# Layer 0 of a four-layer net: three PSUM bank pairs in a ring, both score halves in a row, head mixing behind the product with v

## The chip, the cores and the metric

The kernel runs on one core of a Trainium2 chip. A core has five engines that work beside each other, each through its own instructions in order: TensorE (matmuls; the profile calls it PE and its weight loads PEld), VectorE (DVE), ScalarE (ACT), GpSimd (POOL) and SyncE (SP, which here only issues transfers). Sixteen DMA engines move data. TensorE writes to PSUM, a memory of eight banks of 512 fp32 per partition; ScalarE and VectorE read it. The metric is the time of one execution on the device in microseconds, lower is better. A difference of about 0.2% is what a measurement of this kernel can tell from none.

## The reference

A batch of four images with 512 channels and 32 x 32 positions goes through four residual layers, each on a group-normalized input. The change concerns layer 0, an attention with talking heads:

```python
xf = x.reshape(b, c, t)                         # t = 1024
q, k, v = (einsum('oc,bct->bot', w, xf) ... )   # 8 heads of 64
attn = einsum('bhdq,bhdT->bhqT', q, k) * scale
attn = einsum('gh,bhqT->bgqT', w_head, attn)    # heads mixed before the softmax
attn = softmax(attn, axis=-1)
attn = (attn - mean) / sqrt(var + EPS)          # one mean and var per image and head
attn = attn * in_gamma + in_beta
out = einsum('bhqT,bhdT->bhqd', attn, v)
out = out.reshape(b, t, c) @ w_proj.T + b_proj
```

The layers after it (a small quantum-circuit gate, a second attention, a memory with the best 8 of 2048 items) follow in the same kernel and are not touched. All arithmetic is in fp32.

## The kernel before, in words

Layer 0 works image by image, and an image in 32 steps (`STEPS`) of 32 queries each. `step` (L1164) writes out the order of a step by hand: nearly every instruction goes through `pin` (L55), which keeps the written order on its engine. So what stands first in `step` runs first on its engine, and a waiting instruction holds back everything behind it on that engine.

For one step s the data goes this way:

- `scores(b, s, n)` (L436), for each half n of the keys: eight matmuls of q with k fill a pair of PSUM banks, and ScalarE copies the pair into the SBUF tile `ss`. After the second half the scores are relayed into the tile `s2` (the profile says `s`) by eight DMAs, four issued by SP and four by GpSimd (L462). They turn partitions around so that heads lie beside each other. `s2` has two buffers, so the relay of step s writes where the mixing of step s-2 has read.
- `mix` (L465), two steps later: 16 matmuls with the small matrix `wmix` mix the heads, into two pairs of banks (`mx0`, `mx1`).
- `exps` (L475): ScalarE takes the exponential of each pair into one half of the tile `e`, which has one buffer.
- `turn_keys` (L479): VectorE transposes a half of `e` into `eT`, which has two buffers of four steps each (a tile of 128 queries).
- `reduce` (L488): VectorE takes statistics of `e` (eight `bn_stats`), for the softmax's sums and the variance.
- `apply` (L500): TensorE multiplies `eT` with v into the bank `pv`, in four parts per tile, `LAG` = 6 steps behind the scores. `take_out` (L570) copies the finished bank.
- `sums` (L517): a generator that goes on by a piece at each `next`. GpSimd adds the statistics, TensorE sums them over partitions into the small bank `pt`, VectorE takes the reciprocal, GpSimd sends it through DRAM to spread it (`rb`), and `scale` (L574) multiplies with it on GpSimd.

Eight banks hold all this: the pairs `sc`, `mx0`, `mx1`, and the single banks `pv` and `pt`. Both score halves of a step use the one pair `sc`; the order on TensorE is first scores, mixing of step s-2, second scores, small-bank work, product with v, and then a `piece`.

What fills a `piece` (L1244) depends on the step. In steps 0 to 6 it is `take_v`, the projection of a further tile of v. From step 12 to 27 of images 1 to 3 it is `put_quarter` (L673), a quarter of the output projection of the image before, into the bank `pt`, added to the image by VectorE. In the other steps there is nothing, or small work for the next image's norm. `mid` (L1223) and `early` (L1214) carry further small work: sums of v at steps 7 and 8, the loads of the image pieces `xr` and their stores, the instance norm of the image before, group-norm coefficients, and the loads for the next image, which ScalarE issues in steps 28 to 31. After step 31 come `LAG` steps without scores, four of which hold a q projection of the next image, then its k projections.

Of the kernel before, what the change touches and what calls it, by code (L numbers as in the profile page):

```python
# [10 lines left out]
F32 = mybir.dt.float32  # L11
# [30 lines left out]
def fast_net(ctx: ExitStack, tc: tile.TileContext, a: dict, out: bass.AP, flag: bass.AP):  # L42
# [9 lines left out]
    pairs = {at: ps_a.tile([P, 2, NB], F32, tag=at, name=at) for at in ("sc", "mx0", "mx1")}  # L52
# [124 lines left out]
    def place(at, name):  # L177

        return pairs[at] if at else ps_s.tile([P, 2, NB], F32, tag="sc", name=name)
# [46 lines left out]
    LAG = 6  # L226
# [57 lines left out]
    def first():  # L284
# [35 lines left out]
        def multiply(k, m):  # L320
            for n in range(T // NB):
                pin(nc.tensor.matmul(
                    pairs[f"mx{m}"][:, n, :],
                    w[:, k, m * P:(m + 1) * P], xn[:, k, n * NB:(n + 1) * NB],
                    start=(k == 0), stop=(k == KC - 1),
                ))
# [18 lines left out]
        for m in range(2):  # L345
            put_q(q, m)(flat2(pairs[f"mx{m}"]))
        for m, at in ((2, "sc"), (3, "mx0")):
            project(w, tokens(xn), m, at, put_q(q, m))
# [24 lines left out]
    def normalized(b, scale, bias):  # L373

        xn = img[b]["xn"]
        for ks in ((), (), (0,), (1, 2), (3,)):
            for k in ks:
                pin(nc.scalar.activation(
                    xn[:, k, :], xn[:, k, :], AF.Identity,
                    bias=bias[:, k:k + 1], scale=scale[:, k:k + 1],  # L380
                ))
            yield
# [53 lines left out]
    def scores(b, s, n):  # L436
# [7 lines left out]
        sc = pairs["sc"]  # L444
# [19 lines left out]

    def mix(b, s):  # L465
        s2 = img[b].pop(("s2", s))
        for t in range(4):
            for r in range(4):
                pin(nc.tensor.matmul(  # L469
                    pairs[f"mx{r // 2}"][t * NS:(t + 1) * NS, r % 2, :].rearrange("p (qq k) -> p qq k", qq=2),  # L470
                    wmix[r * NS:(r + 1) * NS], s2[r * NS:(r + 1) * NS, :, t * NK:(t + 1) * NK],
                    start=True, stop=True,
                ))

    def exps(s, half):  # L475
        pin(nc.scalar.activation(  # L476
            e[:, half].rearrange("p r qq k -> p (r qq k)"), flat2(pairs[f"mx{half}"]), AF.Exp))
# [10 lines left out]
    def reduce(b, s):  # L488

        I = img[b]  # L490
        j, i = divmod(s, 4)
        if i == 0:
            I["st", j] = apool.tile([P, 4, 4, 2, 6], F32, tag="st", bufs=2, name=f"st_{b}_{j}")
        st = I["st", j]
        for half in range(2):
            for r in range(2):
                for qq in range(2):
                    pin(nc.vector.bn_stats(st[:, i, 2 * half + r, qq, :], e[:, half, r, qq, :]))  # L498
# [662 lines left out]
    for m, at in enumerate(("mx1", "sc", "mx0", "mx1")):  # L1161
        take_k(0, m, at)

    def step(b, s, mid, piece):  # L1164
# [3 lines left out]
        old = s - 2  # L1168
        j, part = divmod(s - LAG, 4)
        tiled = 0 <= j < TC  # L1170
        if tiled and part == 0:
            I["tail"] = sums(b, j)
            next(I["tail"])
# [5 lines left out]
        if 0 <= old < STEPS:  # L1179
            mix(b, old)  # L1180
            exps(old, 0)
            turn_keys(old, 0)
        elif s < STEPS:
            piece(b, s)
        if s < STEPS:
            scores(b, s, 1)
        if 0 <= old < STEPS:
            exps(old, 1)
        if tiled and part == 0:
            next(I["tail"])  # L1190
        mid(b, s)
        if tiled:
            apply(b, s - LAG)
            if part == 3:
                take_out(b, j)
        if 0 <= old < STEPS:
            turn_keys(old, 1)
            reduce(b, old)
        if old >= 0:
            piece(b, s)  # L1200
        if tiled and part < 3:
            next(I["tail"], None)
# [20 lines left out]
    def mid(b, s):  # L1223
# [5 lines left out]
        if b > 0:  # L1229
            if s == 3:  # L1230
                state["norm"] = instance_norm(before)
            if 3 <= s < 7 or OUT - 2 <= s <= OUT:
                next(state["norm"], None)
            if OUT <= s + 1 < OUT + 16 and s % 2:
                image_piece(before, (s + 1 - OUT) // 4, (s + 1 - OUT) // 2 % 2)
            if OUT < s <= OUT + 16 and s % 2 == 0:
                piece_out(before, (s - 2 - OUT) // 4, (s - 2 - OUT) // 2 % 2)
            if s == NEXT:
                state["behind"] = chain(state["behind"], gating(before))
        if NEXT - 3 <= s:  # L1240
            next(state["ahead"])
        next(state["behind"], None)

    def piece(b, s):  # L1244
# [4 lines left out]
        if TC < s < NEXT - 3 and not state["held"]:  # L1249
            state["held"] = next(state["ahead"]) is True  # L1250

    for b in range(B):
# [12 lines left out]
        places = dict(zip(range(STEPS, STEPS + KC), ("sc", "sc", "mx0", "mx1")))  # L1265
        for s in range(STEPS, STEPS + LAG):
            step(b, s, lambda b, s: next(state["behind"], None),
                 lambda b, s: qs[s - STEPS](places[s]) if s in places else None)
# [5 lines left out]
        for m, at in enumerate(("sc", "mx0", "mx1", "mx0")):  # L1274
            ks[m](at)
        if last:
# [3 lines left out]
            for i, at in enumerate(("mx0", "mx1", "sc", "mx0")):  # L1280
                take_v2(0, i, at)
            for m, at in enumerate(("mx1", "sc", "mx0", "mx1")):
                put_out(b, m, at)
# [799 lines left out]
```

## Time and profile before

| what | value |
|---|---|
| median of 3 runs | 2703.63 us (2702.09 to 2707.51) |
| the profiled execution | 2704.59 us, its span 2702.8 us |
| granted TensorE clock, mean | 0.987 |
| busy: PE, PEld | 2574.9 us (95%), 1143.7 us (42%) |
| busy: DVE, ACT, POOL | 1496.9 (55%), 1007.4 (37%), 1234.5 us (46%) |
| steps of image 0, first scores to last scores' start | 74.12 to 278.19 us |
| the same for images 1, 2, 3 | 358.55 to 589.47, 671.02 to 901.41, 987.08 to 1218.42 us |

Busy time is what the profile shows between an instruction's start and its modelled end; matmuls overlap, so a busy TensorE need not be at its peak. A group of instructions is named by its line, engine, operation and tiles, output before input: `sc<-k,q` are the scores, `mx<-s,wmix` the mixing, `pv<-eT,v` the product with v, `pt<-of,w_p` a projection quarter, `ss<-sc` the copy of scores, `e<-mx` the exponential. Square brackets in a timeline hold the engine's idle time before a row and what ended it. The mean over the span hides that the steps differ; so stretches of it are asked for by themselves.

### The profile page before, as it was taken

The page shows a single profiled execution, that of the slowest core. Times are in us where ns is not written, and L with a number is a line of the kernel's source. Part 1 is how long each engine was busy: PE and PEld are TensorE (multiplying, and loading weights), DVE is VectorE, ACT ScalarE, POOL GpSimd, SP SyncE. Part 2 cuts the span into 40 slices and gives each one's busy share as a digit, 9 for nine tenths or more (in the row PEclk, how much of TensorE's full clock was granted, in tenths as well). Part 3 has the DMA queues.
Part 4 walks back from the last instruction along what each step waited for, and adds up shares of the span by engine and source line. Part 5 has one row for each costly group of instructions (what it writes and reads, how often), then busy time and mean ns, then how long its engine had stood idle before and what let it go on. Part 6 is the DMA issues. An engine that isn't in the chain of part 4 may idle for free.

```text
span 2702.8 us, 47004 instructions
## 1 busy us (share of the span) xinstructions
PE 2574.9 (95%) x18286; PEld 1143.7 (42%) x18286; DVE 1496.9 (55%) x2386; ACT 1007.4 (37%) x1149; POOL 1234.5 (46%) x1891
## 2 busy tenths in 40 slices
PE   8998999989999898989999999999999999999995
PEld 3343434544345443545433443343344344444442
DVE  4497337871588416873246225424513437878886
ACT  1565336551565325652145035214403622121211
POOL 2266425552466415554067027205602626666664
PEclk9999999999999999999999999999999999999997
DMA  2477437770587527675310030021002016766665
GB/s 79 126 212 211 126 94 224 222 217 28 170 234 208 154 67 197 200 209 197 121 44 1 31 125 1 16 81 60 1 32 93 1 56 190 217 190 215 183 183 161
DMA packets 159320, 349.81 MB, mean 129 GB/s; under 512 B 32361, under 2 KB 65129, under 8 KB 155378
## 3 DMA queue, kind: packets, MB, share of 16 engines
q1 hardware_dynamic: 88608, 167.17, 20.1%
q0 software_dynamic: 49152, 142.79, 18.5%
q10 hardware_dynamic: 21330, 36.76, 4.6%
q8 instruction: 147, 2.41, 0.4%
q14 instruction: 83, 0.68, 0.1%
HBM read 178.57 MB, written 33.69 MB: 79 GB/s over the span
## 4 chain that ended last, share of the span: by engine, by line
PE 81%; DMA 6%; ACT 5%; DVE 3%; POOL 2%; issue 2%; SPq 1%; ACTq 0%; POOLq 0%; DVEq 0%
PE at L1096 16%; PE sc_c L975 8%; PE pv_c L1008 8%; PE mx L193 7%; PE sc L447 7%; PE pv L509 6%; DMA s<-ss 4%; PE p L193 4%; ACT ss L453 4%; PE sc L193 4%; PE pt L406 4%; PE q L193 3%; PE k L193 3%; PE v L205 3%; PE pt L682 3%
## 5 line engine op out<-in xcount | busy, mean ns | idle before, releaser
L482 DVE STREAM_TRANSPOSE eT<-e 128x1024 f32<-128x1024 f32 x256 | 316.9, 1241 | 261.5 <-ACT e L476 259.5
L462 POOL DMA_DIRECT2D s<-ss x512 | 259.4, 515 | 364.9 <-ACT ss L453 283.7
L1113 POOL DMA_INDIRECT got<-in_mem,ix x256 | 278.4, 1087 | 217.2 <-DVE tmx L1119 94.1
L453 ACT COPY ss<-sc 128x1024 f32<-128x1024 f32 x256 | 259.0, 1012 | 254.8 <-PE sc L447 205.7
L969 ACT ACTIVATE eT<-sc_c 128x1024 f32<-128x1024 f32 x256 | 247.8, 1022 | 278.8 <-PE sc_c L975 216.9
L498 DVE BATCH_NORM_STATS2 st<-e 128x6 f32<-128x256 f32 x1024 | 341.6, 405 | 0.0
L993 POOL TENSOR_TENSOR e<-eT 128x1024 f32<-128x1024 f32 x96 | 230.1, 2398 | 177.7 <-ACT eT L969 147.0
L447 PE MATMUL sc<-k,q 64*32 64x512 f32 x4096 | 284.0, 610 | 19.8 <-ACT ss L453 14.6
L476 ACT ACTIVATE e<-mx 128x1024 f32<-128x1024 f32 x256 | 262.4, 1028 | 65.2 <-PE mx L469 28.0
L994 DVE TENSOR_TENSOR eT<-eT,e 128x1024 f32<-128x1024 f32 x96 | 131.5, 1370 | 249.5 <-POOL e L993 249.3
L509 PE MATMUL pv<-eT,v 128*64 128x128 f32 x4096 | 254.2, 278 | 0.0
L509 PEld LDWEIGHTS pv<-eT,v 128*64 128x64 f32 x4096 | 223.8, 138 | 61.5 <-issue 59.9
L975 PE MATMUL sc_c<-q,k 64*128 64x512 f32 x1024 | 238.8, 606 | 2.5 <-DVE xr L648 2.3
L989 POOL TENSOR_TENSOR eT<-eT 128x1024 f32<-128x1024 f32 x32 | 80.6, 2520 | 348.6 <-ACT eT L969 335.8
L1008 PE MATMUL pv_c<-eT,v 128*64 128x512 f32 x1024 | 232.2, 596 | 0.0
L469 PE MATMUL mx<-s,wmix 32*32 32x512 f32 x4096 | 157.3, 620 | 39.8 <-DMA s<-ss 39.8
L1137 DVE SCALAR_TENSOR_TENSOR acc<-got,et,acc 128x512 f32<-128x512 f32 x224 | 168.5, 752 | 8.0
L1035 DVE RECIPROCAL ri_c<-ri_c 128x512 f32<-128x512 f32 x32 | 107.1, 3345 | 96.1 <-ACT ri_c L1034 96.1
L975 PEld LDWEIGHTS sc_c<-q,k 64*128 64x128 f32 x1024 | 94.4, 187 | 132.1 <-issue 73.5
L1101 ACT COPY att<-at 128x1024 f32<-128x1024 f32 x64 | 64.8, 1012 | 217.6 <-PE at L1096 217.5
L585 POOL TENSOR_TENSOR o<-pv,rb 64x256 f32<-64x256 f32 x128 | 111.2, 869 | 66.2 <-ACT pv L572 59.2
L1008 PEld LDWEIGHTS pv_c<-eT,v 128*64 128x64 f32 x1024 | 70.5, 137 | 152.6 <-issue 151.4
(316 smaller groups left out, 3231.5 us busy)
## 6 DMA issues: line engine op xcount, KB each, us to landing
s<-ss SPq DMA_DIRECT2D x512, 128.0 KB
s<-ss POOLq DMA_DIRECT2D x512, 128.0 KB, 4.0
rb<-r POOLq DMA_DIRECT2D x64, 128.0 KB, 5.4
o<-o SPq DMA_DIRECT2D x32, 256.0 KB
xr<-in_x ACTq DMA_DIRECT2D x32, 256.0 KB
x<-xr SPq DMA_DIRECT2D x32, 256.0 KB
xr_c<-x SPq DMA_DIRECT2D x32, 256.0 KB
x<-xr_c SPq DMA_DIRECT2D x32, 256.0 KB
```

The lines of the kernel that those rows point to most:

```text
L193: pin(nc.tensor.matmul(ps[:, n, :], w[:, k, m * P:(m + 1) * P], rhs(k, n), start=(k == 0), stop=(k == KC - 1),))
L447: pin(nc.tensor.matmul(sc[m * NS:(m + 1) * NS, r, :], q[r * HD:(r + 1) * HD, m, s * NS:(s + 1) * NS], k_[r * HD:(r + 1) * HD, m, n * NB:(n ...
L453: pin(nc.scalar.copy(ss[:, :, n * NB:(n + 1) * NB], sc))
L462: pin(relays[side].dma_start(out=s2[2 * m + r::NH], in_=ss[m * NS:(m + 1) * NS, r, :]))
L476: pin(nc.scalar.activation(e[:, half].rearrange("p r qq k -> p (r qq k)"), flat2(pairs[f"mx{half}"]), AF.Exp))
L482: pin(nc.vector.transpose(eT[:, j % 2].rearrange("p b (qq i r) x -> p i r qq b x", qq=2, i=4)[:, i, 2 * half:2 * half + 2], e[:, half].rea ...
L498: pin(nc.vector.bn_stats(st[:, i, 2 * half + r, qq, :], e[:, half, r, qq, :]))
L509: pin(nc.tensor.matmul(pv[r * HD:(r + 1) * HD, gp, :], I["v"][:, t, g * HD:(g + 1) * HD], eT[:, j % 2, t, :, 4 * g:4 * g + 4], start=(t == ...
L975: pin(nc.tensor.matmul(sc[:, r, :], I["k"][r * HD:(r + 1) * HD, m, t * P:(t + 1) * P], I["q"][r * HD:(r + 1) * HD, m, n * NB:(n + 1) * NB] ...
L1008: pin(nc.tensor.matmul(pv[r * HD:(r + 1) * HD, :], I["v"][:, t, h * HD:(h + 1) * HD], e[:, r, :], start=(t == 0), stop=(t == TC - 1),))
L1096: pin(nc.tensor.matmul(sc[:, n * NB:(n + 1) * NB], xn3[b][:, k, tt * P:(tt + 1) * P], memT[k][:, i0:i0 + NB], start=(k == 0), stop=(k == K ...
L1113: pin(nc.gpsimd.indirect_dma_start(out=got[:, i, :], out_offset=None, in_=a["mem"], in_offset=bass.IndirectOffsetOnAxis(ap=ix[:, i:i + 1], ...
```

## The change

Three things are reordered, with no matmul added or left out.

The three pairs of banks become a ring without fixed roles. Score half n of step s takes pair (s+n) mod 3; the mixed half h in step s takes pair (s+2+h) mod 3. So within a step the second mixed half reuses the pair of the first scores, and the next step's second scores reuse the pair of the first mixed half.

The order in a step is now: both score halves; the sums matmul; in steps with a projection quarter, `mid`; the product with v; the mixing; both exponentials; in other steps `mid`; the `piece`.

VectorE's work for the second half of `e` (transpose and four statistics) is put off to the next step, behind that step's small-bank work. Because of that, the sums of a tile begin at step 4j+6 and their matmul stands in step 4j+7, and the product lags by 7 steps instead of 6. The copy of `pv` stands behind both exponentials. The store of an image piece (`piece_out`) moves to the start of a step, its load (`image_piece`) behind the copy of `pv`, and the small norm work for the next image starts one step earlier.

```diff
-    pairs = {at: ps_a.tile([P, 2, NB], F32, tag=at, name=at) for at in ("sc", "mx0", "mx1")}
+    pairs = [ps_a.tile([P, 2, NB], F32, tag=f"pair{i}", name=f"pair{i}") for i in range(3)]
...
-    LAG = 6
+    MIX = 2
+    SUM = 6
+    LAG = 7
...
-        sc = pairs["sc"]
+        sc = pairs[(s + n) % 3]
...
+    def mixed(s, half):
+        return pairs[(s + MIX + 2 + half) % 3]
...
     def step(b, s, mid, piece):
         I = img[b]
-        old = s - 2
+        old = s - MIX
+        mixing = 0 <= old < STEPS
+        js, at = divmod(s - SUM, 4)
+        summing = 0 <= js < TC
         j, part = divmod(s - LAG, 4)
         tiled = 0 <= j < TC
-        if tiled and part == 0:
-            I["tail"] = sums(b, j)
-            next(I["tail"])
+        putting = b > 0 and OUT <= s < OUT + 16
+        if b > 0 and OUT < s <= OUT + 16 and s % 2 == 0:
+            piece_out(b - 1, (s - 2 - OUT) // 4, (s - 2 - OUT) // 2 % 2)
         if s == 0:
             take_v(b, 0)
         if s < STEPS:
             scores(b, s, 0)
             early(b, s)
-        if 0 <= old < STEPS:
+            scores(b, s, 1)
+        if summing and at == 1:
+            next(I["tail"])
+        if putting:
+            mid(b, s)
+        if s >= MIX and "late" in I:
+            turn_keys(I["late"], 1)
+            reduce(b, I.pop("late"), 1)
+        if summing and at == 0:
+            I["tail"] = sums(b, js)
+            next(I["tail"])
+        if tiled:
+            apply(b, s - LAG)
+        else:
+            piece(b, s)
+        if mixing:
             mix(b, old)
             exps(old, 0)
+            exps(old, 1)
             turn_keys(old, 0)
-        elif s < STEPS:
-            piece(b, s)
-        if s < STEPS:
-            scores(b, s, 1)
-        if 0 <= old < STEPS:
-            exps(old, 1)
-        if tiled and part == 0:
-            next(I["tail"])
-        mid(b, s)
-        if tiled:
-            apply(b, s - LAG)
-            if part == 3:
-                take_out(b, j)
-        if 0 <= old < STEPS:
-            turn_keys(old, 1)
-            reduce(b, old)
-        if old >= 0:
-            piece(b, s)
-        if tiled and part < 3:
+        if tiled and part == 3:
+            take_out(b, j)
+        if b > 0 and OUT <= s + 1 < OUT + 16 and s % 2:
+            image_piece(b - 1, (s + 1 - OUT) // 4, (s + 1 - OUT) // 2 % 2)
+        if not putting:
+            mid(b, s)
+        if tiled:
+            piece(b, s)
+        if mixing:
+            reduce(b, old, 0)
+            I["late"] = old
+        if summing and at > 0:
             next(I["tail"], None)
```

The rest of the diff gives the projections of q, k and v and the first image's start their places in the ring by number, gives `reduce` the half as an argument, and moves the two image-piece calls out of `mid`.

## The prediction, made before the changed kernel ran

> **What bounds the kernel now.** I read the page first: TensorE is busy 95% of the span, so a change must either take TensorE's waits away or shorten its sequence. The change touches layer 0 alone, which the timeline puts between 74 and about 1290 us. So I asked next for TensorE's waits in that stretch:
>
> ```profile
> PE mx L469 <- DMA s<-ss: 39.8, 18, 6.5
> PE pt L533 <- POOL sums L530: 14.8, 12, 2.2
> PE sc L447 <- ACT ss L453: 14.6, 19, 1.5
> ```
>
> The columns are total us, times, longest. The mixing waits for its relayed scores, the small sums matmul for GpSimd, the scores for ScalarE's copy of the half before. All rows together give about 78 us: what waiting alone could return. Then the timeline of one step of image 1 with a projection quarter, TensorE's rows and the copy:
>
> ```profile
> 460.54 1.09 PE L447 MATMUL sc<-k,q 64*32 64x512 f32 x16
> ...
> 461.55 1.20 PE L469 MATMUL mx<-s,wmix 32*32 32x512 f32 x32
> 461.73 1.01 ACT L453 COPY ss<-sc 128x1024 f32<-128x1024 f32 x1 [2.36 <-PE sc L447]
> ...
> 462.80 1.09 PE L447 MATMUL sc<-k,q 64*32 64x512 f32 x16
> 462.90 1.02 ACT L476 ACTIVATE e<-mx 128x1024 f32<-128x1024 f32 x1 [0.15 <-PE mx L469]
> ```
>
> Start to start: first scores 1.02, mixing 1.24, second scores 1.02, product with v 1.90, quarter 1.93: 7.11 us, and most of steps 13 to 24 of images 1 to 3 take exactly that. Such steps are TensorE's own length, hardly any waiting. "Bare" steps, with neither a projection nor a quarter (image 0 from step 9; steps 9 to 11 and 28 to 31 elsewhere), are 5.18 at best. In image 0 they are far from it, and one call with stretches shows why; columns are length, busy PE, PEld, DVE, ACT, POOL, then clock, DMA share, GB/s:
>
> ```profile
> 149.75:248.50 98.75, 87.73 (x1580) 42.74 (x1579) 89.93 (x186) 65.42 (x70) 71.65 (x158) 0.98 0.76 222
> 570.00:575.00 5.00, 4.96 (x96) 2.32 (x96) 4.46 (x12) 3.33 (x4) 3.33 (x10) 1.00 1.06 256
> 575.00:580.00 5.00, 1.29 (x20) 0.19 (x16) 4.45 (x10) 1.83 (x3) 2.18 (x4) 0.99 1.05 262
> 580.00:585.00 5.00, 2.70 (x40) 0.57 (x48) 0.22 (x1) 1.51 (x2) 2.81 (x7) 0.50 0.75 221
> ```
>
> VectorE is 91% busy in image 0; and where the next image's loads run (570 to 580) the DMA engines are full, TensorE stands still, and its clock is 0.50 after that. One more row, from image 0, for the sums:
>
> ```profile
> 172.71 0.41 PE L533 MATMUL pt<-sums,same 128*128 128x32 f32 x2 [1.59 <-POOL sums L530]
> ```
>
> The second scores began at 170.00, so this matmul comes 2.71 after them instead of 1.02.
>
> **What the skill says.** TensorEngine Tiling (Array Packing), Key Properties: a change of tiling mode drains TensorE. The trace agrees: the scores' second pass starts 0.453 after the first and would leave the array free 0.91 after the block's start, yet the mixing (other tile shape) comes at 1.02. TensorE: Matmul & The Clock Gate, Part 1: after an idle window of about 3.4 us the clock is halved. It agrees: after 5.73 us of waiting the mixing at 582.30 took 2.02 instead of 1.20. DMA: Bandwidth & Descriptors, Anatomy of one DMA: a semaphore wait for a DMA is done on the issuing sequencer. So GpSimd's queue stands still while a relay waits; GpSimd's 283.7 us of waits for the copy, on the page, fit.
>
> **The change, part by part**, summed against the profiled run (2704.6 us, span 2702.8; median of the runs 2703.6, so the same within 0.04%).
>
> (a) *Scores side by side.* One mode change of five goes (1.02 to 0.91: 0.11), and the wait of second scores for the first copy goes. The mixing's second pass would free the array at about 1.04, with a drain of 0.11 at 1.15; it now takes 1.24: 0.09. Step with a quarter: 0.91+1.02+1.90+1.15+1.93 = 6.91, so 0.20 less. 48 such steps (12 to 27 of three images): -9.6.
>
> (b) *Steps 0 and 1* have no mixing to lie between the score halves. TensorE waits 1.17 us for the copy at each step's end, from 78.77 to 81.03. With the ring: 0.91+1.02+3.63 (v) = 5.56 for 6.91: -1.35 x 8 = -10.8.
>
> (c) *A new wait.* The second scores take the pair that the previous step's first mixed half leaves, so they wait for its exponential. That begins 1.35 after the mixing's start (461.55 to 462.90), takes 1.02, and 0.06 later scores may start: 2.43 after the mixing. With the quarter between they come only at 1.15+1.93+0.91 = 3.99: hidden. In a bare step they would come at 2.06: 0.37 of stall, and the loop is 2.43+1.02+1.90 = 5.35, over 5.18. In steps 2 to 6 (v instead of the product) 2.43+1.02+3.63 = 7.08 for 6.95: +0.13 x 20 = +2.6. Steps 7 and 8 have the sums of v behind the mixing, which hides it: -0.15 x 8 = -1.2.
>
> (d) *Sums a step later.* GpSimd adds in step 4j+6, the matmul stands behind the next step's scores, VectorE's second half and its statistics are done early. The 14.8 us should nearly go. In bare steps 0.3 stays: GpSimd issues four relays (2.0) before the add (0.29), done about 2.4 after the mixing's end, where the matmul would come at 2.25.
>
> (e) *Bare steps of image 0.* Steps 9 to 28 took 120.25 us, 6.01 each. VectorE needs 89.93 in the 16 steps of the stretch shown with a small edge, near 5.5 each; the loop of (c) 5.35 plus a quarter of sums (0.33+0.3) and of the pv copy (0.59), which now stands behind both exponentials: 5.65. I take 5.70: -0.31 x 20 = -6.2. Bounds: 5.5 (-10) and no gain.
>
> (f) *Relays.* Their issue now waits for the mixing of two steps before, later in the same step; in return the mixing is late too. Issue on GpSimd 2.05, landing median 4.0, longest 9.5 (page and tile view). Time from the end of one mixing to the next use of its buffer: 2 x 6.91 - 1.2 = 12.6, less 2.3 of issue and signals leaves 10.3 for landing. Before, copy end (4.45 into the step) to mixing two steps on (1.02): 8.4. In bare steps: 2 x 5.5 - 3.6 = 7.4 against about 5. So about 2 us more room. Queued behind the waiting relay are, on GpSimd, the sums and the scaling (some 2.3 us a step, waited for by TensorE in (d) only), on SP the stores of o and x, which none waits for soon. Steps 9 to 11 of images 1 to 3 took 61.9 us, 7.9 of it DMA waits in TensorE's list; at 5.7 and half the waits 55.3: -6.6. Steps 28 to 31: the mixing of step 30 waits 4.7 to 6.6 us, and stands 2.8 later in its step, which would take 2.8 and some of the slow clock; but the engines are full there, so half of 14 comes back in the next step: -7. Bounds 0 and -20.
>
> (g) *Small-bank work and sums in the quarter steps.* Those 48 steps take 353.7; at 7.11 they are 341.3, plus 4 of sums matmuls: 8.4 is waits and small matmuls around steps 12, 22 and 25 to 28. I let 40% go: -3.4. VectorE needs 88.67 us of 103.34 there, 6.1 of 7.1 a step, so 6.9 is still open to it. The image piece is now loaded behind the exponentials: 7 us before its add instead of 12, which the landing times cover.
>
> (h) One step more of lag adds no instructions to TensorE's tail, where projections fill it: 0. If the product had to wait for VectorE at steps 35 to 38 it would cost some 1 us per image. The bank names in the first and last projections: 0, the copies there have 7 us projections as cover.
>
> Sum: -9.6-10.8+2.6-1.2-6.2-6.6-7.0-3.4 = -42.2, so 2661.4 of the median; I say 2662.
>
> **Rivals.** *The freed time is taken back*: VectorE at 91% and full DMA engines set the pace, so (e), (f) give nothing and (a), (g) half: -10.8+1.4-6.5 = -16, 2688. For it: the stretches shown. Against it: VectorE's 5.5 is under 6.01, and its second half is now ready work for idle moments.
>
> *The DMA waits go*: 2.8 us more room ends the half clock too; (f) gives 20 and 10, (e) 10: -62, 2642. For it: each wait is a single event per image. Against: the engines are already full at 262 GB/s there.
>
> *Slower*: the ring ties TensorE to VectorE. Its place is the first exponential, which waits for `e` to be read (25.6 us of such waits before), and the second scores now wait for that exponential without the whole step that lay between. If VectorE's delays add to the 5.35 loop, the 44 bare steps grow. Gains (a) and (b), less the rest of (c), are 19, and (g)'s 3.4: 22.4 in all, so it decides from 0.5 us per bare step over before, at about 6.5 in image 0; at 7.0 it is +22, 2726. For it: image 0 runs at 6.01 with a floor of 5.18, so adding happens already. Against: the second half no longer stands between two first halves.
>
> That the change does not do what it says is excluded: in the built order TensorE has both score halves, product, mixing, quarter.
>
> **How the numbers follow.** Forecast 0.58 (2645 to 2680), taken back 0.18 (2680 to 2698), waits gone 0.09 (2638 to 2645), no change 0.05, slower 0.10. About 0.2%, 5 us, is what a measurement can tell from no change. Range 2640 to 2697: it leaves out most of the slower case and some of no change. Faster 0.85, same 0.05, slower 0.10.
>
> **What would show it.** Step starts 6.9 apart with quarters, 5.6 in steps 0 and 1, near 5.7 in bare steps of image 0; no scores row waiting for the copy, a new one waiting for the exponential, some 0.3 each in bare and v steps; sums under 4 us; DMA waits of the mixing near 25 instead of 39.8. I am wrong if the exponential's row passes 30 us, if VectorE is idle while bare steps stay at 6.0, or if the relays land later and the DMA row grows.

## The result, and the profile after

The changed kernel takes 2700.89 us, median of 20 runs (2690.16 to 2705.93), where the kernel before took 2704.90, median of 20 runs beside them (2699.03 to 2713.91). The ratio is 0.9978, 95% interval 0.9968 to 0.9989: some 6 us faster, just about what can be measured. The forecast was 2662, with a range of 2640 to 2697: the kernel gave back nearly all of what it should have gained.

First the page of the changed kernel, busy time, share of the span and instructions of each engine:

```profile
PE 2581.5 (96%) x18286; PEld 1156.0 (43%) x18286; DVE 1483.1 (55%) x2387; ACT 996.4 (37%) x1148; POOL 1236.2 (46%) x1891
```

TensorE has the same 18286 matmuls and is busy 6.6 us *longer* than before. The mean clock of this profiled execution is 0.979, that of the one before 0.987, but the two lie at the edges of what the kernels show. Over its 20 runs the changed kernel has 0.979 to 0.983, median 0.9815. The kernel before has 0.982 to 0.987, median 0.984, in the 15 runs made beside the first experiments. By the medians the loss of clock is 0.0025 of 2702 us, some 7 us of work (an estimate); the two profiles alone would make it 22.

The list of TensorE's waits in layer 0 (74 to 1300 us) has the same columns as before, total us, times, longest:

```profile
PE pair L475 <- DMA s<-ss: 29.7, 11, 4.8
PE pt L538 <- POOL sums L535: 20.3, 10, 5.1
PE pair L449 <- ACT e L482: 9.5, 38, 1.5
```

The mixing's waits for relayed scores fell, from 39.8 to 29.7. The scores' wait for the exponential is the new one of step (c), at 0.25 each time. But the row of the sums, which was to go nearly to nothing, grew from 14.8 to 20.3, and its longest wait from 2.2 to 5.1. The sum of all rows is 78.3 us, as before. The list does not hold every stop, though: it has those between TensorE's matmuls, and a matmul's modelled end can hide a stop inside a block.

Such a stop came with the ring. The mixing's second half now writes the pair that the first scores of the same step used, so it waits for ScalarE's copy of them. It is seen in the list of TensorE's weight loads, before and then after:

```profile
PEld mx L469 <- ACT ss L453: 1.7, 1, 1.7
```

```profile
PEld pair L475 <- ACT ss L455: 14.5, 26, 0.9
```

One step of image 1 with a projection quarter, in the timeline:

```profile
519.59 1.95 PE L449 MATMUL pair<-k,q 64*32 64x512 f32 x32
521.47 1.97 PE L514 MATMUL pv<-eT,v 128*64 128x128 f32 x32
523.36 1.14 PE L475 MATMUL pair<-s,wmix 32*32 32x512 f32 x32
524.43 1.99 PE L687 MATMUL pt<-of,w_p 128*128 128x256 f32 x8
...
526.36 1.09 PE L449 MATMUL pair<-k,q 64*32 64x512 f32 x16
```

From start to start: both score halves 1.88, product 1.89, mixing 1.07, quarter 1.93: 6.77 us where it was 7.11. That is 0.34 less a step, where (a) had forecast 0.20.

So I cut the span at the starts of scores and put stretch beside stretch. All numbers are us, each from one profiled execution, sums over the images named:

| stretch | before | after | forecast | measured |
|---|---|---|---|---|
| up to the first scores | 74.1 | 74.1 | 0 | 0.0 |
| steps 0 and 1, all images | 55.3 | 44.1 | -10.8 | -11.2 |
| steps 2 to 8, all images | 211.7 | 203.8 | +1.4 | -7.9, less 7.6 moved: -0.3 |
| steps 9 to 28, image 0 | 120.2 | 125.2 | -6.2 | +5.0 |
| steps 9 to 11, images 1 to 3 | 61.9 | 73.7 | -6.6 | +11.8 |
| steps 12 to 27, images 1 to 3 | 353.7 | 337.6 | -13.0 | -16.1 |
| from there to the next image or the end | 1825.9 | 1843.6 | -7.0 | +17.7, less 7.6 moved: +10.1 |
| span | 2702.8 | 2702.0 | -42.2 | -0.8 |

The 7.6 us are bookkeeping: with one step more of lag the product starts a step later, so one product per image (1.89 us) leaves steps 2 to 8 and stands behind step 31. The two rows have to be read together with it. The untouched layers at the end of the last row hardly move (1344.9 us before, 1343.2 after, from the second attention's first scores).

The table says where to look. What TensorE's own sequence was to give came in full: steps 0 and 1 and the quarter steps give 27 us. All of it was lost again where no quarter stands behind the mixing: in the bare steps 9 to 28 of image 0, 9 to 11 of the others, and at the ends. In image 0 two steps carry the loss: 26 and 27 took 22.7 us where they took 14.9, while the other 18 gave 2.8. So these two are the place to look at, in windows (columns as before):

```profile
236.00:242.00 6.00, 3.91 (x55) 1.95 (x47) 4.80 (x10) 2.07 (x3) 5.21 (x13) 1.00 1.01 262
242.00:250.00 8.00, 4.89 (x62) 1.38 (x62) 2.70 (x6) 5.19 (x6) 3.24 (x10) 0.75 0.57 120
250.00:258.00 8.00, 6.04 (x82) 4.25 (x82) 2.74 (x6) 0.52 (x1) 6.84 (x14) 0.61 0.28 66
```

In the first window the DMA engines are full at 262 GB/s, as they were before in the stretches with the next image's loads. But in the 16 us behind it they have almost nothing to do (share 0.57, then 0.28), VectorE works a third of the time, and TensorE is slow all the same. None of these is the limit there; the engines wait for each other. The timeline shows how, from somewhat earlier on:

```profile
232.19 0.20 POOL L151 TENSOR_TENSOR dm_a<-mv_a,gm_a 128x4 f32<-128x4 f32 x1 [4.32 <-DVE gm_a L131]
...
234.78 2.05 POOL L464 DMA_DIRECT2D s<-ss  x4
...
240.94 2.65 PE L475 MATMUL pair<-s,wmix 32*32 32x512 f32 x32 [2.09 <-DMA s<-ss]
241.98 0.23 PEld L475 LDWEIGHTS pair<-s,wmix 32*32 32x32 f32 x28 [0.90 <-ACT ss L455]
243.52 0.59 PE L156 MATMUL pt<-gsq_a,gavg 128*128 128x4 f32 x2
246.10 1.05 POOL L120 TENSOR_TENSOR grstd_a<-gve_a,mhalf 128x4 f32<-128x4 f32 x1 [4.33 <-DVE gve_a L162]
249.53 2.07 POOL L464 DMA_DIRECT2D s<-ss  x4 [0.50 <-issue]
251.61 0.30 POOL L535 TENSOR_TENSOR sums<-st 128x32 f32<-128x32 f32 x1
251.96 0.64 PE L538 MATMUL pt<-sums,same 128*128 128x32 f32 x2 [5.07 <-POOL sums L535]
252.53 3.68 PE L514 MATMUL pv<-eT,v 128*64 128x128 f32 x32
256.14 1.14 PE L475 MATMUL pair<-s,wmix 32*32 32x512 f32 x32
```

Read it from the end. The product at 252.53 runs at about half speed (3.68 instead of 1.97), since TensorE has just waited 5.07 us for the sums. The sums' add on GpSimd (251.61) stands behind the four relay instructions of its step, which take 2.07 us (249.53). That relay did not wait for its buffer. The mixing of 240.94 had read it by 243.6, GpSimd came to the relay 5.9 us later, and only 0.50 us of idle time lies before it.

What kept GpSimd is small norm work for the next image: `grstd_a` (246.10) waited 4.33 us for VectorE. VectorE's value comes from the small matmul at 243.52, which stands behind the late mixing. That mixing was late for a like reason: `dm_a` (232.19) had held GpSimd for 4.32 us, so step 24's relay was issued at 234.78, though the mixing had freed its buffer at 229.2, and it then shared the full DMA engines with the loads. In its own middle this mixing stopped once more for the copy of the scores (241.98), and its last matmuls ran slow.

So it is a loop. A late mixing makes late norm work on GpSimd, this a late relay and late sums, these a late product, and the product now stands *ahead of* the next mixing. From mixing to mixing it takes 15.2 us instead of some 5.4.

The other long waits for the sums, in step 31 of images 1 to 3, look alike: 3.18, 4.45 and 3.17 us, behind a norm instruction that had waited 10.37, 7.03 and 9.28 us for VectorE, and a relay with under 0.5 us of idle time before it. The first of them:

```profile
595.56 1.04 POOL L120 TENSOR_TENSOR grstd_b<-gve_b,mhalf 128x4 f32<-128x4 f32 x1 [10.37 <-DVE gve_b L162]
```

These four make 15.9 of the 20.3 us. In the other six the relay had waited for its buffer, 1.2 to 5.1 us, and TensorE then lost 0.65 to 0.78 us each, 4.4 in all. Before the change, the add stood ahead of that norm instruction (in image 0 the add at 244.45, `grstd_a` at 253.42). Among the changes is that the norm work starts a step earlier, and this puts it in front.

### The profile page after: what moved, and what is told of

It is laid out like the page before. It is cut to its first block, busy times and chain, and to the rows that moved or that the text cites. A ratio compares the mean times of both kernels' runs of the same rounds, so it can differ in the third digit from the quotient of the medians.

```text
span 2702.0 us, 47106 instructions
## 1 busy us (share of the span) xinstructions
PE 2581.5 (96%) x18286; PEld 1156.0 (43%) x18286; DVE 1483.1 (55%) x2387; ACT 996.4 (37%) x1148; POOL 1236.2 (46%) x1891
## 4 chain that ended last, share of the span: by engine, by line
PE 79%; DMA 5%; DVE 2%; ACT 1%; issue 1%; ACTq 0%; POOL 0%; SPq 0%; POOLq 0%
PE at L1101 16%; PE pair L193 9%; PE sc_c L980 9%; PE pv_c L1013 8%; PE pv L514 5%; PE pair L449 5%; PE p L193 4%; PE pair L475 4%; PE pt L408 3%; PE pt L687 3%; PE k L193 3%; PE q L193 3%; PE v L205 3%; DMA s<-ss 3%; PE rs_c L1034 1%
## 5 line engine op out<-in xcount | busy, mean ns | idle before, releaser
L503 DVE BATCH_NORM_STATS2 st<-e 128x6 f32<-128x256 f32 x1024 | 350.3, 403 | 1.9 <-POOL sqs L567 1.9
L482 ACT ACTIVATE e<-pair 128x1024 f32<-128x1024 f32 x256 | 250.5, 1023 | 201.0 <-PE pair L475 179.6
L455 ACT COPY ss<-pair 128x1024 f32<-128x1024 f32 x256 | 249.4, 1019 | 143.2 <-DMA s<-ss 64.9
L449 PE MATMUL pair<-k,q 64*32 64x512 f32 x4096 | 271.4, 618 | 18.7 <-ACT e L482 9.5
L475 PE MATMUL pair<-s,wmix 32*32 32x512 f32 x4096 | 171.1, 630 | 37.1 <-DMA s<-ss 29.7
L449 PEld LDWEIGHTS pair<-k,q 64*32 64x32 f32 x4096 | 59.2, 107 | 186.2 <-ACT e L482 75.3
```

Source lines behind the costliest of these rows:

```text
L449: pin(nc.tensor.matmul(sc[m * NS:(m + 1) * NS, r, :], q[r * HD:(r + 1) * HD, m, s * NS:(s + 1) * NS], k_[r * HD:(r + 1) * HD, m, n * NB:(n ...
L475: pin(nc.tensor.matmul(mixed(s, r // 2)[t * NS:(t + 1) * NS, r % 2, :].rearrange("p (qq k) -> p qq k", qq=2), wmix[r * NS:(r + 1) * NS], s ...
L482: pin(nc.scalar.activation(e[:, half].rearrange("p r qq k -> p (r qq k)"), flat2(mixed(s, half)), AF.Exp))
```

## Experiments

Three theories stood against each other. **A**: a relay now waits for a mixing that stands behind the product, and since instructions are written in order, it holds back what is written behind it on GpSimd, the sums above all. **B**: the DMA engines' bytes are the limit, wherever the instructions stand. **C**: putting VectorE's second half off to the next step makes its results late. Later a fourth joined them, **L**: the loads for later work, which stand between the two score halves, hold back the relays. None of them names the norm work that the timeline shows ahead of the sums, and no run moves it. All stretches below are from one profiled execution each.

### A third buffer where there is room

In steps 9 to 25 of image 0 a piece of SBUF, the memory in which the tiles lie, is free (that of a later weight). Every third relay there goes into it, which takes the relays' wait for the mixing away without moving an instruction.

```diff
-        s2 = I["s2", s] = apool.tile([P, 2, T], F32, tag="s2", bufs=2, name=f"s2_{b}_{s}")
+        if b == 0 and 9 <= s < 26 and s % 3 == 0:
+            s2 = I["s2", s] = eight_k([P, 2, T], f"s2_{b}_{s}", 2)
+        else:
+            s2 = I["s2", s] = apool.tile([P, 2, T], F32, tag="s2", bufs=2, name=f"s2_{b}_{s}")
```

> The changed kernel; in image 0, steps 9 to 25, every third relay goes into a third buffer (the weight slot w2, idle there), so that no relay of steps 9 to 24 waits for the mixing of its own step. Nothing else differs. Theory A, relays that wait for the mixing behind the product start late, hold up GpSimd's queue, and make the long waits: image 0 from the start of step 9 to that of step 29 falls from 125.2 us to 115 or less, SyncE's waits for the mixing fall by about 17 of their 110 times, and the whole gains 8 to 12 us on the changed kernel. Theory B, the DMA engines are full and the freed time is only taken back by them: the stretch stays at 124 to 126. Theory C, VectorE's put-off half sets the pace of image 0: 123 to 126.

Measured: 2693.01, ratio to before 0.9955 (0.9938 to 0.9972), some 6 us better than the changed kernel by the ratios. Steps 9 to 28 of image 0 took 120.1 us for 125.2.

SyncE's relays waited for the mixing 93 times instead of 110, as expected, and 5.1 us are gone with it. The stretch had lost 5.0 against the kernel before, so this brings it back there, and not to the 114 that was forecast or the 115 expected of this run. Most of the gain is in one step: step 26 took 5.66 us for 9.53. The long wait for the sums in step 27 stayed, at 4.7 us. Steps 9 to 11 of images 1 to 3 took 66.9 for 73.7 too, which cannot come from the edit itself, since it touches image 0 only. As that stretch differs by 7 us between two kernels with the same code there, I read nothing from it alone.

### The relay's instructions written behind the mixing

Nothing else moves: the eight relay DMAs are written behind `turn_keys(old, 0)` instead of behind the second scores. So on GpSimd the sums' add, and in quarter steps the work in `mid`, stand in front of the relay that they stood behind.

```diff
+    def relay(b, s):
...
         if mixing:
             mix(b, old)
             exps(old, 0)
             exps(old, 1)
             turn_keys(old, 0)
+        if s < STEPS:
+            relay(b, s)
```

> The changed kernel with the relay's DMA instructions written behind the mixing instead of behind the second scores. They can hardly start earlier than that anyway; but GpSimd does the sums add and what else stands in the step before it blocks. Theory A in the form that GpSimd's blocked queue is what counts: TensorE's wait for the sums falls from 20.3 us to under 6, the long stops at step 27 of image 0 go, 8 to 15 us off the whole. Theory A in the form that the late start of the transfers counts: sums under 6, but the mixing's DMA wait stays near 30 or grows, under 5 us off the whole. Theories B and C: no change beyond 3 us.

Measured: 2677.48, ratio 0.9900 (0.9875 to 0.9925): a version that beats both kernels, by more than the 8 to 15 us that were expected. TensorE's waits:

```profile
PE pair L476 <- DMA s<-ss: 25.5, 9, 5.7
...
PE pt L539 <- POOL sums L536: 9.1, 4, 3.0
```

The sums fell from 20.3 to 9.1 (under 6 was expected), though the relays were written later, not earlier, and all rows together from 78.3 to 63.2. The timeline at the same place of image 0:

```profile
236.61 3.05 PE L476 MATMUL pair<-s,wmix 32*32 32x512 f32 x32 [2.15 <-DMA s<-ss]
242.26 1.05 POOL L120 TENSOR_TENSOR grstd_a<-gve_a,mhalf 128x4 f32<-128x4 f32 x1 [4.87 <-DVE gve_a L162]
245.15 0.29 POOL L536 TENSOR_TENSOR sums<-st 128x32 f32<-128x32 f32 x1
245.49 0.41 PE L539 MATMUL pt<-sums,same 128*128 128x32 f32 x2 [3.01 <-POOL sums L536]
245.69 2.07 POOL L465 DMA_DIRECT2D s<-ss  x4 [0.26 <-issue]
245.83 1.97 PE L515 MATMUL pv<-eT,v 128*64 128x128 f32 x32
247.72 1.14 PE L476 MATMUL pair<-s,wmix 32*32 32x512 f32 x32
```

It begins the same way, with a mixing that is late and slow, and GpSimd waits as long for the small norm work. But the add at 245.15 is now ahead of the relay: TensorE stops for 3.01 instead of 5.07, its clock is full again at the product (1.97, not 3.68), and the next mixing is there after 11.1 us instead of 15.2. The stretch of image 0 took 118.2 for 125.2, 4.5 of these 7 us in step 27. The larger part of the gain lies at the ends of the images, 1830.3 us for 1843.6. The six short waits for the sums are gone; the four long ones are left, 1.9 to 3.0 us each, still behind the norm work.

### Only GpSimd's half of it

SyncE's four relays stay in their old place, GpSimd's four move (shown against the version before this one).

```diff
+        relay(s2, ss, 0)
+        I["relay"] = s2, ss
...
         if s < STEPS:
-            relay(b, s)
+            relay(*I.pop("relay"), 1)
```

> The changed kernel with GpSimd's four relay issues written behind the sums add and the mixing, while SyncE's four stay behind the second scores. If the order on GpSimd is what the later relays mended: 2674 to 2685, sums wait under 12 us, as with all eight moved. If it was the order on SyncE, or of SyncE's relays against ScalarE's loads: 2695 to 2703, as the changed kernel.

Measured: 2683.68, ratio 0.9882 (0.9847 to 0.9916), the same gain within the interval. The waits:

```profile
PE pair L478 <- DMA s<-ss: 36.9, 13, 6.0
PE pt L541 <- POOL sums L538: 7.5, 4, 2.4
```

So it is the order on GpSimd that counts: what it costs to have the relay in front of the sums and of `mid`. Of theory A the half that speaks of SyncE is not needed.

### Both together

The third buffer in image 0, and the relay written later.

```diff
+        if b == 0 and 9 <= s < 26 and s % 3 == 0:
+            s2 = I["s2", s] = eight_k([P, 2, T], f"s2_{b}_{s}", 2)
...
+        if s < STEPS:
+            relay(b, s)
```

> Relays written behind the mixing, and the third buffer in image 0. If the third buffer helped through the earlier start of the transfers, which this order of GpSimd's and SyncE's instructions still allows: image 0 from step 9 to 29 falls from 118.2 to 114 or less, the whole to 2670 to 2675. If it helped only because GpSimd was not held in front of the sums, the two gains are the same gain: 117 to 119, the whole 2675 to 2680.

Measured: 2679.78, ratio 0.9890 (0.9861 to 0.9918), image 0's stretch 120.4 for 118.2 with the later relay alone. The gains do not add. One loss taken away twice would look like this, but the steps do not say so: the third buffer alone had shortened step 26, the later relay alone step 27, and with both, step 26 took 9.36 us again. Why is open.

### The relay at the very end of the step

```diff
             next(I["scale"])
+        if s < STEPS:
+            relay(b, s)
```

> The changed kernel with the relay's instructions at the very end of the step: now all of GpSimd's work of a step (sums, their follow-up, scaling, norm) stands in front of its relays, not only the sums add. Theory A, form blocked queue: TensorE's sums wait at 5 or less and 2 to 8 us under the run with the relays behind the mixing. Theory A, form late transfers: the relays now also wait for VectorE's results behind GpSimd's work, the mixing's DMA wait grows by 10 or more and the whole is 5 to 15 us over that run.

Measured: 2719.36, ratio 1.0031 (1.0019 to 1.0043). In TensorE's waits the row of GpSimd's sums is gone altogether, and another has grown:

```profile
PE pair L476 <- DMA s<-ss: 48.6, 14, 7.6
```

The quarter steps, undisturbed in the changed kernel, took 357.2 for 337.6. Here the relays land late. So the relay can stand too early in a step, in front of work that others wait for, and too late, so that it has not landed for the mixing two steps on.

### The second half not put off

```diff
-        if s >= MIX and "late" in I:
-            turn_keys(I["late"], 1)
-            reduce(b, I.pop("late"), 1)
...
         if mixing:
+            turn_keys(old, 1)
             reduce(b, old, 0)
-            I["late"] = old
+            reduce(b, old, 1)
```

> The changed kernel with VectorE's second half (transpose and statistics) back in its own step instead of the next. Theory C, the put-off half makes VectorE late and so the exponentials and sums: the whole gains 5 to 15 us, image 0 from step 9 to 29 falls under 120. Theory A: the put-off half is innocent or a help; the whole stays within 5 us or loses up to 15, since the second half then stands between two first halves. Theory B: no change.

Measured: 2706.68, ratio 0.9994 (0.9982 to 1.0006), some 4 us slower than the changed kernel by the ratios, whose intervals overlap a little. The wait for the sums rose to 25.4 us in 15 places. As the cause of the loss, theory C falls: without the put-off half image 0 is no faster (127.6 for 125.2), and the quarter steps lose 12 us (349.7 for 337.6). Steps 9 to 11 took 64.7 for 73.7, in the stretch from which nothing can be read alone.

### The loads later in the step

`early`, with the loads for later work, moves from between the score halves to behind the exponentials; then the same together with the later relay.

```diff
         if s < STEPS:
             scores(b, s, 0)
-            early(b, s)
             scores(b, s, 1)
...
             turn_keys(old, 0)
+        if s < STEPS:
+            early(b, s)
```

> The changed kernel with the loads that ScalarE issues in steps 7 to 10 and 28 to 31 written behind the exponentials instead of between the two score halves. Theory L, in these stretches the copy of the second scores and SyncE's relays stand behind slow load issues: steps 9 to 12 of images 1 to 3 fall from 73.7 us to 66 or less, SyncE's waits for loads fall from 55 us to under 30, the whole gains 5 to 15 us. Theory B, the bytes bound these stretches: they stay within 2 us, only their order changes. Theory A, with GpSimd's order as the cause: within 3 us as well.

> Relays written behind the mixing, which gave 2677 us, and the loads behind the exponentials. If both causes are real and separate, the gains add: 5 to 12 us under 2677, steps 9 to 12 of images 1 to 3 at 63 or less. If the loads' bytes bound the rest: 2675 to 2680.

Measured: 2729.56, ratio 1.0059 (1.0042 to 1.0076), and with the later relay 2696.96, 0.9945 (0.9926 to 0.9965), worse than the later relay alone. In the first, the projections of the next image wait for their weights, 12.6 us in 5 places. The ends of images 1 and 2, from step 31 on, took 202.0 us for 179.2. Their steps 28 to 30, with those of image 3, became shorter, 53.8 for 67.9, which fits loads that compete with the relays; but what is held back there is missing in the next stretch. So moving the loads back within the step does not pay, and theory L does not explain the loss.

### Loads of image 0 moved to the middle of the image

If bytes are the limit at the ends, moving them must move the time. On top of the later relay, the next image's loads are issued from step 14 of image 0 on instead of from step 28.

```diff
-        if s == NEXT:
+        if s == (NEXT if b else 14):
```

> Relays written behind the mixing, and the 3 MB of loads for image 1, which run in steps 28 to 31 of image 0, begin at step 14 instead. Theory B for the ends, the loads' bytes beside the relays bind there: from step 29 of image 0 to image 1 falls from 101.5 us to 94 or less, step 9 to 29 rises by less than that. If the ends are long for another reason: 100 to 103.

Measured: 2681.58, ratio 0.9900 (0.9872 to 0.9929), no change from the later relay alone. The end of image 0 took 92.9 us for 101.5, its steps 9 to 28 128.5 for 118.2: 8.6 gained, 10.3 lost. Between these two places the loads cost about what they free, as theory B says. The run cannot tell whether by their bytes or by holding back the relays.

### The mixing back in front of the product, in bare steps

If the relay waits for a late mixing, an earlier mixing should free it. In all steps without a quarter the mixing is written ahead of the product.

```diff
+        if putting:
+            product()
         if mixing:
             mix(b, old)
             exps(old, 0)
             exps(old, 1)
+        if not putting:
+            product()
+        if mixing:
             turn_keys(old, 0)
```

A first version had the first half's transpose ahead of the product too. In steps 4j+10 this writes into the tile whose last quarter the product still has to read, so it multiplies part of a later tile instead, which makes its result wrong, and waits for that tile's transpose.

```diff
             turn_keys(old, 0)
+        if not behind:
+            product()
```

> The changed kernel, but in all steps without a projection quarter the mixing stands directly behind the scores again, in front of the product with v (or of v's projection); quarter steps stay as changed. Theory A: the relay's wait for the mixing there ends about 1.9 us sooner, image 0 from step 9 to 29 falls from 125.2 to 116 or less, steps 9 to 12 of images 1 to 3 from 73.7 to about 62, the ends of the images give back some 10, and the whole is 25 to 40 us under the changed kernel, near 2665. The second mixed half now waits for the copy of the first scores, some 0.3 us per such step, in place of the scores' wait for the exponential. Theory B: within 5 us of the changed kernel. Theory C: within 5 us.

> As the run with the mixing in front of the product, but the first half's transpose is written behind the product, so that the product no longer waits for it. The rest as there: quarter steps unchanged, in other steps scores, mixing, exponentials, product. Theory A in the form that a relay's late start counts: image 0 from step 9 to 29 at 117 or less, steps 9 to 12 at 64 or less, the whole 15 to 30 us under the changed kernel. Theory A in the form that only the sums behind the blocked relay count: a relay blocks GpSimd 1.9 us less, so the sums wait falls to 5 to 12 and the whole by 5 to 12 us. Theory B: within 5 us.

The first version (the diff just above, `behind` being `putting`) took 2725.83, ratio 1.0070 (1.0053 to 1.0087), with 42.2 us of the product's waits for `eT`, which the changed kernel doesn't have, so it says nothing on the question. The second took 2699.71, ratio 0.9964 (0.9951 to 0.9976), not to be told apart from the changed kernel by these intervals:

```profile
PE pair L475 <- DMA s<-ss: 33.1, 14, 5.5
PE pt L538 <- POOL sums L535: 14.5, 4, 5.2
```

With the mixing first the relay's buffer is free sooner and the sums wait less, but they still stand behind it. What this order costs shows in the weight loads: the mixing's second half waits for the copy of the first scores in 63 places, 26.6 us, where it was 26 places and 14.5. The last run adds the later relay to this order:

```diff
         if mixing:
             turn_keys(old, 0)
+        if s < STEPS:
+            relay(b, s)
```

> Mixing in front of the product in steps without a quarter, and the relays written behind the sums add and the mixing. If GpSimd's order explains the loss and the earlier relay helps besides: sums wait under 8 us, image 0 from step 9 to 29 at 117 or less, the whole 2665 to 2675. If the earlier relay is worth nothing once the sums stand in front: 2674 to 2682, as the run with the relays behind the mixing alone.

Measured: 2694.26, ratio 0.9955 (0.9934 to 0.9976). The sums' row falls to 9.3 us and the mixing's rises to 35.9. The mixing behind the product is therefore not what costs: with the relay in its better place the changed kernel's order is the faster one (0.9900).

### What the runs leave

| kernel | median us | ratio to before | sums wait | mixing waits for DMA | clock of the profiled run |
|---|---|---|---|---|---|
| changed | 2700.89 | 0.9978 | 20.3 | 29.7 | 0.979 |
| third buffer, image 0 | 2693.01 | 0.9955 | 18.4 | 20.8 | 0.983 |
| relay later | 2677.48 | 0.9900 | 9.1 | 25.5 | 0.985 |
| GpSimd's relays later | 2683.68 | 0.9882 | 7.5 | 36.9 | 0.982 |
| relay at the end | 2719.36 | 1.0031 | none | 48.6 | 0.982 |

Shown: that the relay's place on GpSimd, ahead of the sums and of `mid`, costs 0.8 to 1.0 of the 1.3 points (hundredths of the time before) by which the forecast was missed (two kernels take it away by order alone; the ratios compared are each to the kernel before, run beside it). Shown for image 0: that its end's loads moved to step 14 cost there about what they free at the end.

Not shown, but read from traces: that the norm work ahead of the sums makes the four long waits. A run with the norm work back in its later step would test it. Open: the rest of the miss, some 10 to 15 us by the runs with the later relay. Two things of that size are left in them, the four waits behind the norm work (9.1 and 7.5 us) and the stops in the middle of the mixing (12.5 and 14.4). Open too: why the stretch of steps 9 to 11, 61.9 before, took 73.7 us in the changed kernel, 66.9 with the third buffer, and 69.9 and 75.0 with the later relays.

## Why the prediction was wrong

Its main claim, that TensorE's own sequence gets shorter by so much, held. The loss lies in the steps that have no filling. The step of the prediction that failed is (d), with the sentence of (f) that leans on it: that GpSimd would be on time for the sums.

- **(a) scores side by side**: right. A quarter step is 6.77 us where 6.91 was forecast. The second scores follow after 0.88 (0.91 forecast) and the mixing to the quarter takes 1.07 (1.15): the end of the mixing was priced too high by 0.08. Over 48 steps 0.34 is 16.3 us for the 9.6 forecast.
- **(b) steps 0 and 1**: right, 5.51 each for 5.56, -11.2 for -10.8.
- **(c) the new wait for the exponential**: right in place, and nearly in size. In bare steps with nothing else the second scores start 2.42 after the mixing (2.43) and the step takes 5.34 (5.35); the row is 9.5 us over 38 waits. A step with v takes 7.07 (7.08). Steps 2 to 8 together, to gain 1.4 us in length, are 0.3 shorter once the moved products are taken out. The ring's other new wait, of the mixing's second half for the copy of the first scores, is in no term: 14.5 us in 26 places.
- **(d) sums a step later**: this is the step that failed. "The 14.8 us should nearly go" was reckoned from a GpSimd that is on time: the relay's 2 us of issue, then the add, so that 0.3 us remain. The row grew to 20.3. In most steps the matmul does not wait, and in six it waits 0.7 us, behind a relay that had waited for its buffer. But in four it waits 3.2 to 5.1 us. There, as the traces read, small norm work for the next image, which the change starts a step earlier, holds GpSimd in front of relay and add. The prediction gives that move no term, and no reason for leaving it out.
- **(f) relays**: wrong. It named what is queued behind the relay on GpSimd, "waited for by TensorE in (d) only", and took that as settled there. With the relay written behind the add, 0.8 to 1.0 points come back. "About 2 us more room" for the landing is there, and shows: the mixing's waits for the relay fell to 29.7, where 25 was forecast. But steps 9 to 11 lost 11.8 where 6.6 was to be gained, and the ends lost 10.1 where 7 was.
- **(e) bare steps of image 0**: wrong, +5.0 for -6.2, and steps 26 and 27 alone are +7.8. With the relay behind the sums the stretch is at 118.2, 5.91 each: 2 us of the 6.2 gained. The 5.70 was a sum of TensorE's loop in undisturbed steps, which runs at 5.34. What holds the rest no run isolates; moving loads into this stretch cost 10.3 us, so transfers are tight there as well.
- **(g) small-bank work**: not seen. Steps 12 to 27 gave 16.1 us for the 13.0 of (a) and (g) together, but (a) alone makes 16.3 of it. What these steps take over 48 undisturbed ones was 12.4 us before and is 12.6 now, so the sum came out near by luck: (a) was priced too low, and (g) gave nothing. The put-off half does carry something, since without it the quarter steps take 12 us more.
- **(h) one step more of lag**: right, 7.6 us change place, and steps 2 to 8 less this are as before.

The prediction took the sum of waits, 78 us, as "what waiting alone could return". What a stop costs is more than the stop. The Trainium skill, TensorE: Matmul & The Clock Gate, Part 1, was used for the half clock after an idle window of about 3.4 us, and it agrees here: after 5.07 us without a matmul the product took 3.68 for 1.97. Somewhat shorter waits slowed the work as well: after one of 2.99 us (441.33) the mixing's matmuls took 1.03 to 1.06 us each, where 0.61 is usual at full clock. And a part of the stops is not in that sum at all. The 4096 matmuls of the mixing are busy 171.1 us after the change and were busy 157.3 before, while an undisturbed block of 32 became *shorter* with the change, 1.14 for 1.20. So the blocks are some 25 us over 128 undisturbed ones, where they were some 4 over. That is both kinds: the stops of the second half (14.5 us by the weight loads) and blocks at slow clock. With the later relay the blocks are still busy 165.8 us.

Of the rivals, "the freed time is taken back" (2688) was nearest in kind, but not as it was argued. In the worst 16 us of image 0 VectorE and the DMA engines were mostly idle, though the stretch that led into them had the engines full, and GpSimd twice waited over 4 us for a small result of VectorE. "Slower" had named the right sort of cause, a tie of TensorE to a slower engine that adds up round the loop, and the wrong place for it: the exponential's row stayed at 9.5 us, far under the 30 that would have spoken for it.

## What to carry to other kernels

When the order of instructions changes, write down for each in-order queue what now stands in front of a result that a busy engine waits for, the small work too, and ask what each of these waits for. If the chain ends at the busy engine's own later work, it is a loop, and a delay in it goes round instead of being absorbed. Here the cure for a part of it cost nothing: the transfer was written behind the small add that TensorE waits for (0.8 points), yet not at the end of the step, where it is late itself. And compare kernels by stretches between fixed points, with work that only changed its stretch taken out, before looking for a cause; a median alone would have said here that nothing happened, where 27 us were gained and nearly all lost again.

## What was unexpected of the hardware

**A stop that counts as busy.** TensorE's waits in layer 0 came to 78.3 us in both kernels, but the list has only stops between matmuls. A mixing that stops in its middle counts as busy right through. The one at 146.48 ran at full clock and took 2.07 us instead of 1.14: after its first four matmuls its weight load waited for ScalarE's copy. The list of the weight loads is where such stops show.

**A relay that seems to wait for another's load.** At steps 9 to 11 of image 1 SyncE's third relay of a step was issued at 445.52, 11 us after the second, and its list of waits names a weight's load, not the mixing (before, the longest of these was 3.2):

```profile
SPq L464 <- DMA w_p<-in_w_proj: 22.1, 6, 10.0
```

The mixing then waited until 453.58, and the DMA engines' share between 452 and 457 was 0.16. Neither the code nor the data makes that relay depend on the weight. The profile infers who ended a wait, so the name may be wrong; the late issue is not in doubt. No run tests its cause.
